# A two-layer pre-activation convolution: the order of ScalarE's work in a step, and statistics taken ahead

## The chip, the cores and the metric

The kernel runs on one core of one Trainium2 chip. The metric is the device time of one execution in microseconds. The kernel before takes 1926.62 us (median of three runs, 1925.54 to 1932.41). The profile shown here is of one execution of 1926.6 us from its first to its last instruction.

## What is computed

The input x has 8 images of 32 channels and 252 by 252 pixels, in fp32. Two layers of the same kind follow each other:

```python
def _gn(v, G=16, eps=1e-5):                  # group norm, 2 channels a group
    g = v.reshape(B_, G, C_ // G, H_, W_)
    m = jnp.mean(g, axis=(2, 3, 4), keepdims=True)
    s = jnp.var(g, axis=(2, 3, 4), keepdims=True)
    return ((g - m) / jnp.sqrt(s + eps)).reshape(v.shape)

x = x + _L0_conv_ref(_gn(x), L0_conv_weight)   # 5x5 convolution, 32 -> 32,
x = x + _L1_conv_ref(_gn(x), L1_conv_weight)   # reflected borders
```

A convolution of layer 1 on an image can start only when the mean and variance of the whole image behind layer 0 are known. The reference writes the convolution as a product of Fourier transforms; the kernel computes it directly.

## The kernel before

**Tiles.** An image is split into even and odd rows and columns, which gives four parts of 126 by 126 pixels. With 32 channels each they fill the 128 partitions. The 5x5 convolution becomes a convolution with three column taps, and along the rows a fast scheme that makes six output rows from eight transformed rows: 8 products instead of 18. One step works on a tile of 18 rows of the parts: 7 steps an image and layer, 112 steps in all.

**Phases.** `phases` (L500) lists (image, layer) pairs: layer 0 of image 0, then layer 0 of image b alternating with layer 1 of image b-1, then layer 1 of the last image: 16 phases of 7 steps. `s0` is the first step of a phase in `begin`.

**One step on each engine**, in the order of the loop at L581, for step i:

- SyncE issues all DMAs, in program order: `fetch` (L106) loads the rows of step i+4 of layer 0 into one of two halves of `xbuf`; `prepare` (L141) loads the tile `g` of step i+3 from a DRAM scratch if it is of layer 1; stores of the step before go to the scratch (L464) or to the output (L497); `input_chunk` (L267) loads parts of an image for its sums.
- GpSimd runs `differences` (L346) for step i+2: three subtractions and additions, a dependency keeps the first behind VectorE's last instruction of `transform`.
- VectorE runs `transform` (L359) for step i+1, then `finish` (L448) of step i-1, then, in `conv` (L405), s1 and d1 (L423, L424: they read m2 and a1), the pair at L431 and L432 (they read m3, m4, a3), six results y (L397), the pair at L440 and L441 (m5, m6, a5), four more y.
- TensorE runs the products m3, m4, m5, m6 of step i, then `first_products` (L401), that is m1 and m2 of step i+1, and then products 0 and 7 of step i on top of m6 and m5. Each is three matmuls of 128x378 (two instructions each in the trace, 48 a step). Products 0 and 7 write where VectorE reads m6 and m5, and so wait for the last y of L443.
- ScalarE copies a1, a3 and a5 from the PSUM (L420, L427, L437) for VectorE, and beside these it does four other kinds of work: splitting the rows of step i+3 into the tile `g` if it is of layer 0 (`prepare`, L154 to L156, through `after_1`, behind a1); the first half of the output of step i-1, or its borders and sum (`after_3`, behind a3); the second half or sum of squares (`after_5`, behind a5); sums and sums of squares of an image to come (`input_sums`, L274, also in `after_5`).

The order within an engine is the program's (`manual_schedule`, L526); every engine runs its list from top to bottom. PSUM holds seven product tiles and one small tile for statistics.

**Statistics of a phase.** `collect` (L288) adds up the partial sums, `averages` (L293) is a small matmul across partitions, `variance` (L299) ends in a square root on ScalarE, `scales` (L310) makes the factors, `scale_matrices` (L327) multiplies the phase's matrices `u` on ScalarE, `add_own` (L331) adds the residual to them on VectorE, and `find_offset` (L336) makes the offset that a1 takes as its bias. Before the change `collect` and `averages` run in step s0-2, all else in step s0-1 (`mid` and `late`, L523 and L524). The input sums of a layer-0 phase run in steps s0-7 to s0-4.

Of the kernel before, what the change touches and what calls it, by code (L numbers as in the profile page):

```python
# [46 lines left out]
F32 = mybir.dt.float32  # L47
# [5 lines left out]
P = 128  # L53
Q = 32
EPS = 1e-5
NB = 126
PB = 128
TR = 6
NT = 3
# [15 lines left out]
def tile_conv_preact_x2(ctx: ExitStack, tc: tile.TileContext, x: bass.AP, w0: bass.AP, w1: bass.AP, out: bass.AP):  # L75
# [65 lines left out]
    def prepare(b: int, l: int, T: int):  # L141

        g = gpool.tile([P, DR, NT, PB], F32, tag="g", name=f"g_{b}_{l}_{T}")
        gt[b, l, T] = g
        if l:
            nc.sync.dma_start(g[:, 0:TR], scratch[b][:, T])
            nc.sync.dma_start(g[:, TR:DR, 0 : NT - 1], scratch[b][:, T, 0:2, 1:NT])
            nc.sync.dma_start(g[:, TR:DR, NT - 1], scratch[b][:, T + 1, 0:2, 0])
            return
        t = xt.pop((b, T))  # L150
        for pc in range(2):
            cols = slice(1 - pc, W, 2)
            to = g[halves[pc], :, :, 1 - pc : 1 - pc + NB]
            nc.scalar.copy(to[:, 0:TR], t[:, 0:GR, cols].rearrange("p (t j) w -> p j t w", j=TR))  # L154
            nc.scalar.copy(to[:, TR:DR], t[:, 2:IR, cols].rearrange("p (t j) w -> p j t w", j=TR)[:, TR - 2 : TR])  # L155
        pad_columns(g.rearrange("p j t k -> p (j t k)"), 0)  # L156
# [125 lines left out]
    def output_sums(b: int, T: int, y: bass.AP, k: int):  # L282
        st = sum_slots(b, 1)
        view = y[:, 0 : GR * PB].rearrange("p (r k) -> p r k", k=PB)[:, :, 1 : 1 + NB]
        junk = spool.tile([P, GR, NB], BF16, tag="junk", name=f"junk_{b}_{T}_{k}", bufs=1)
        nc.scalar.activation(junk, view, (AF.Identity, AF.Square)[k], accum_out=st[:, k, T : T + 1])  # L286
# [44 lines left out]
    def add_own(b: int, l: int):  # L331
        u = ut[b, l]
        for pc, h in enumerate(halves):
            last["dve"] = nc.vector.tensor_add(u[h, :, 1 + pc, h], u[h, :, 1 + pc, h], own[h])

    def find_offset(b: int, l: int):  # L336
        po = pstat.tile([P, 1], F32, tag="stat", name=f"po_{b}_{l}")
        nc.tensor.matmul(po, total[l], norm.pop((b, l))[:, 1:2], start=True, stop=True)
        offset[b, l] = small.tile([P, 1], F32, tag="off", name=f"off_{b}_{l}")
        nc.scalar.copy(offset[b, l], po)  # L340


    at, vt = {}, {}
# [57 lines left out]
    def first_products(b: int, l: int, T: int):  # L401
        n = f"{b}_{l}_{T}"
        m12[b, l, T] = [product(b, l, vt[b, l, T], f, n) for f in (1, 2)]

    def conv(b: int, l: int, T: int, after_1, after_3, after_5, following):  # L405

        vs = vt[b, l, T]
        n = f"{b}_{l}_{T}"

        y = ybuf[begin[b, l] + T & 1]  # L410
        yr = y[:, 0 : GR * PB].rearrange("p (j t k) -> p j t k", j=TR, k=PB)
        yo = [yr[:, j, :, 1 : 1 + NB] for j in range(TR)]

        def temp(tag: str, bufs: int = 1):
            return mpool.tile([P, NT, NB], F32, tag=tag, name=f"{tag}_{n}", bufs=bufs)

        v = nc.vector
        m1, m2 = m12.pop((b, l, T))
        a1 = temp("a1", 2)
        nc.scalar.activation(a1, m1, AF.Identity, bias=offset[b, l])  # L420
        after_1()
        s1, d1 = temp("s1"), temp("d1")
        v.tensor_add(s1, m2, a1)  # L423
        v.tensor_sub(d1, a1, m2)  # L424
        m3 = product(b, l, vs, 3, n)
        a3 = temp("a3", 2)
        nc.scalar.copy(a3, m3)  # L427
        after_3()
        m4 = product(b, l, vs, 4, n)

        v.tensor_sub(m3, a3, m4)  # L431
        v.tensor_add(m4, m4, a3)  # L432
        for j in (1, 0, 3, 2, 5, 4):
            stt(yo[j], m3 if j % 2 else m4, 2.0**j, d1 if j % 2 else s1)
        m5 = product(b, l, vs, 5, n)
        a5 = temp("a5", 2)
        nc.scalar.copy(a5, m5)  # L437
        after_5()
        m6 = product(b, l, vs, 6, n)
        v.tensor_sub(m5, a5, m6)  # L440
        v.tensor_add(m6, m6, a5)  # L441
        for j in range(1, 5):
            stt(yo[j], m5 if j % 2 else m6, 0.5**j, yo[j])  # L443
        following()
        product(b, l, vs, 0, n, m6)
        product(b, l, vt.pop((b, l, T)), 7, n, m5)

        def finish():  # L448
            v.tensor_add(yo[0], m6, yo[0])
            stt(yo[5], m5, 0.5**5, yo[5])  # L450

        return y, finish
# [28 lines left out]
    def to_output(b: int, T: int, y: bass.AP, s: int):  # L481

        yr = y[:, 0 : GR * PB].rearrange("p (j t k) -> p j t k", j=TR, k=PB)
        if s == 0:
            ot[b, T] = opool.tile([P, half, W], F32, tag="o", name=f"o_{b}_{T}")
        o = ot[b, T] if s == 0 else ot.pop((b, T))
        o = o.rearrange("p (t j) w -> p t j w", j=TR // 2)
        js = slice(s * TR // 2, (s + 1) * TR // 2)
        dst = out[b].rearrange("ch (i r) w -> r ch i w", r=2)[:, :, GR * T : GR * (T + 1), :]
        dst = dst.rearrange("r ch (t j) w -> r ch t j w", j=TR)  # L490
        for pc in range(2):
            nc.scalar.copy(  # L492
                o[halves[s], :, :, 1 - pc : W : 2].rearrange("p t j w -> p j t w"), yr[halves[pc], js, :, 1 : 1 + NB]
            )
        for pr in range(2):
            for t in range(NT):
                nc.sync.dma_start(dst[1 - pr, :, t, js, :], o[quads[2 * s + pr], t])  # L497
# [8 lines left out]
    N = len(steps)  # L506


    chunk_load: dict = {}
    chunk_sum: dict = {}  # L510
    mid: dict = {}
    late: dict = {}
    for k, (p, s0) in enumerate(begin.items()):
        ut[p] = ubuf[(k + 1) % 2]
        if k == 0:
            continue
        b, l = p
        if l == 0:
            for c in range(NC):
                at_step = s0 - 7 + c // 2 if k > 1 else c * 5 // 8  # L520
                chunk_sum.setdefault(at_step, []).append((b, c))
                chunk_load.setdefault(at_step - 1, []).append((b, c))
        mid.setdefault(s0 - 2, []).append(p)  # L523
        late.setdefault(s0 - 1, []).append(p)  # L524

    ctx.enter_context(tc.manual_schedule())  # L526
    beside = mybir.DependencyInfo(mybir.DependencyClass.Sync, mybir.DependencyReason.DATA)
# [39 lines left out]
    add_own(0, 0)  # L567
    find_offset(0, 0)
    first_products(*steps[0])
    next(first)  # L570
    prepare(*steps[1])
    differences(nc.gpsimd, *steps[1])
# [2 lines left out]
    transform_taps(taps_at[:, 1], rows_at, rsum)  # L575
    sum_taps(1, taps_at[:, 1])

    for b, c in chunk_load.get(-1, []):
        chunks[b, c] = input_chunk(b, c)
    done = None  # L580
    for i, step in enumerate(steps):  # L581
        if i + 4 < N:
            fetch(*steps[i + 4])
        for p in mid.get(i, []):
            nc.sync.dma_start(ut[p], stored[p[1]])
            collect(*p)
        for p in late.get(i, []):
            variance(*p)
        parts = transform(*steps[i + 1]) if i + 1 < N else iter(())
        next(parts, None)  # L590
        for p in late.get(i, []):
            scales(*p)
            scale_matrices(*p)
        next(parts, None)
        for p in late.get(i, []):
            add_own(*p)
        if done:
            done[2]()
        if i + 2 < N:
            first = differences(nc.gpsimd, *steps[i + 2])  # L600
            tc.add_manual_dep(first.ins, last["dve"].ins.name, beside, reason="one reader of two operands at a time")

        def after_1():
            if i + 3 < N:
                prepare(*steps[i + 3])

        def after_3():
            if done:
                (b, l, T), y, _ = done
                if l:  # L610
                    to_output(b, T, y, 0)
                else:
                    to_scratch(b, T, y)
                    output_sums(b, T, y, 0)

        def after_5():
            if done:
                (b, l, T), y, _ = done
                if l:
                    to_output(b, T, y, 1)  # L620
                else:
                    output_sums(b, T, y, 1)
            for b, c in chunk_sum.get(i, []):
                input_sums(b, c, chunks.pop((b, c)))
            for b, c in chunk_load.get(i, []):
                chunks[b, c] = input_chunk(b, c)

        def following():
            for p in mid.get(i, []):
                averages(*p)  # L630
            for p in late.get(i, []):
                find_offset(*p)
            if i + 1 < N:
                first_products(*steps[i + 1])

        done = step, *conv(*step, after_1, after_3, after_5, following)
        if i == 1:
            make_matrices(1, rows_at, ubuf[0])
    done[2]()
# [34 lines left out]
```

## Time and profile before

| What | us |
|---|---|
| span | 1926.6 |
| TensorE busy, matmuls | 1762.5 (91%) |
| VectorE busy | 1729.5 (90%) |
| ScalarE busy | 1377.4 (71%) |
| GpSimd busy | 827.9 (43%) |
| TensorE's first product | starts at 51.9 |
| TensorE waits for VectorE's y | 88.7 in 26 waits, the longest 8.1 |
| VectorE waits at L431 for a3 | 69.9 in 15 waits, the longest 6.3 |
| ScalarE waits for m3 at L427 | 264.2 in 62 waits |
| DMA | 386.4 MB, mean 201 GB/s |

Two engines are busy nine tenths of the time and feed each other within every step, so a mean share says little here. What matters is in which steps they wait, and for whom; that is read from the timeline and from the distance of one instruction to the same instruction of the next step.

### The profile page before, as it was taken

To read this page: it belongs to the slowest core of one execution; us is meant where nothing else is said; L and a number is where in the kernel's file an instruction comes from. 1 tells how busy PE (TensorE), PEld (TensorE's weight loads), DVE (VectorE), ACT (ScalarE), POOL (GpSimd) and SP (SyncE) were. 2 spreads that over 40 slices of the span, in tenths; PEclk is the share of its full clock that TensorE was granted. 3 is DMA by queue.
4 is the path that set the end of the run, shared out by engine and by line. 5 is a ranking of instruction groups with operands and counts; after the bars stand their busy time and mean duration, and the time that the engine had idled before them with its cause. 6 is when DMAs were issued, how large, how long until landed. Compare 5 with 4: busy or idle time off the path is not lost.

```text
span 1926.6 us, 19376 instructions
## 1 busy us (share of the span) xinstructions
PE 1762.5 (91%) x5440; PEld 1041.3 (54%) x5440; DVE 1729.5 (90%) x3345; ACT 1377.4 (71%) x1649; POOL 827.9 (43%) x410
## 2 busy tenths in 40 slices
PE   0579999999999899999999999999999989999997
PEld 0345555555555455555555555555555545555554
DVE  6677899988999799988999889998899889999995
ACT  5779774988669885797847977498856988444443
POOL 5643344434444344444444434443444434444440
PEclk9789999999999999998999999999999999999999
DMA  6959768996679786797778966899767977766653
GB/s 221 237 152 223 140 142 243 285 227 139 177 232 289 171 169 196 242 262 168 147 204 302 239 147 150 245 281 226 151 180 240 278 172 156 205 173 195 180 148 87
DMA packets 225660, 386.39 MB, mean 201 GB/s; under 512 B 25488, under 2 KB 200848, under 8 KB 212624
## 3 DMA queue, kind: packets, MB, share of 16 engines
q1 hardware_dynamic: 225552, 385.16, 76.2%
q8 instruction: 42, 0.69, 0.2%
q14 instruction: 66, 0.54, 0.1%
HBM read 249.77 MB, written 135.28 MB: 200 GB/s over the span
## 4 chain that ended last, share of the span: by engine, by line
PE 55%; DVE 18%; ACT 12%; DMA 8%; issue 4%; POOL 2%; SPq 2%; ACTq 0%; DVEq 0%; POOLq 0%
PE m L387 55%; DVE y L397 8%; ACT g L154 4%; DMA x<-in_x_dram 3%; DMA out_dram<-o 1%; ACT g L155 1%; DMA g<-scratch 1%; DVE v L368 1%; ACT sx L279 1%; ACT o L492 1%; ACT sx L280 1%; DMA sx<-in_x_dram 1%; DVE m L440 1%; DVE m L432 1%; DVE m L441 1%
## 5 line engine op out<-in xcount | busy, mean ns | idle before, releaser
L387 PE MATMUL m<-v,u 128*128 128x378 f32 x5376 | 1761.3, 489 | 105.2 <-DVE y L397 88.7
L387 PEld LDWEIGHTS m<-v,u 128*128 128x128 f32 x5376 | 1031.4, 193 | 818.0 <-DVE y L397 104.7
L354 POOL TENSOR_TENSOR a<-g 128x1536 f32<-128x1536 f32 x111 | 384.4, 3463 | 1042.2 <-DVE v L368 414.7
L492 ACT COPY o<-y 64x1134 f32<-64x1134 f32 x224 | 278.3, 1242 | 12.2 <-issue 8.5
L397 DVE SCALAR_TENSOR_TENSOR y<-m,y 128x378 f32<-128x378 f32 x560 | 275.5, 542 | 2.9 <-PE m L387 2.9
L154 ACT COPY g<-x 64x2268 f32<-64x2268 f32 x112 | 256.6, 2291 | 11.9 <-DMA x<-in_x_dram 9.8
L427 ACT COPY a<-m 128x378 f32<-128x378 f32 x112 | 53.1, 474 | 266.4 <-PE m L387 264.2
L286 ACT ACTIVATE junk<-y 128x2268 bf16<-128x2268 f32 x112 | 234.7, 2096 | 1.4
L356 POOL TENSOR_TENSOR v<-g 128x768 f32<-128x768 f32 x111 | 202.6, 1825 | 0.0
L355 POOL TENSOR_TENSOR e<-g 128x768 f32<-128x768 f32 x111 | 202.6, 1825 | 0.0
L397 DVE SCALAR_TENSOR_TENSOR y<-m,d 128x378 f32<-128x378 f32 x336 | 182.1, 542 | 0.0
L397 DVE SCALAR_TENSOR_TENSOR y<-m,s 128x378 f32<-128x378 f32 x336 | 182.1, 542 | 0.0
L431 DVE TENSOR_TENSOR m<-a,m 128x378 f32<-128x378 f32 x112 | 62.2, 556 | 125.0 <-ACT a L427 69.9
L280 ACT ACTIVATE sx<-sx 128x2016 f32<-128x2016 f32 x64 | 118.9, 1857 | 19.7 <-DVE sums L277 17.4
L368 DVE SCALAR_TENSOR_TENSOR e<-g,e 128x768 f32<-128x768 f32 x112 | 108.5, 969 | 9.2 <-POOL e L355 9.2
L368 DVE SCALAR_TENSOR_TENSOR v<-p 128x384 f32<-128x384 f32 x224 | 115.2, 556 | 0.0
L368 DVE SCALAR_TENSOR_TENSOR v<-q 128x384 f32<-128x384 f32 x224 | 115.0, 555 | 0.0
L368 DVE SCALAR_TENSOR_TENSOR p<-a 128x768 f32<-128x768 f32 x112 | 107.2, 958 | 0.0
L368 DVE SCALAR_TENSOR_TENSOR q<-a 128x768 f32<-128x768 f32 x112 | 106.8, 954 | 0.0
L368 DVE SCALAR_TENSOR_TENSOR v<-a,v 128x768 f32<-128x768 f32 x112 | 106.6, 952 | 0.0
L279 ACT ACTIVATE sx<-sx 128x2016 f32<-128x2016 f32 (+1 forms) x56 | 103.5, 1848 | 0.5
L420 ACT ACTIVATE a<-m,off 128x378 f32<-128x378 f32 x112 | 63.7, 569 | 51.5 <-PE m L387 50.8
(67 smaller groups left out, 972.0 us busy)
## 6 DMA issues: line engine op xcount, KB each, us to landing
g<-scratch SPq DMA_DIRECT2D x56, 1152.0 KB, 8.9
out_dram<-o SPq DMA_DIRECT2D x672, 94.5 KB, 2.0
sx<-in_x_dram SPq DMA_DIRECT2D x56, 1008.0 KB, 5.8
x<-in_x_dram SPq DMA_DIRECT2D x88, 630.0 KB, 8.5
scratch<-y SPq DMA_DIRECT2D x112, 288.0 KB, 2.8
scratch<-y SPq DMA_DIRECT2D x112, 240.0 KB, 3.6
u<-raw SPq DMA_DIRECT2D x15, 1536.0 KB, 7.1
g<-scratch SPq DMA_DIRECT2D x56, 256.0 KB, 9.2
```

The costliest lines, as they stand in the source:

```text
L154: nc.scalar.copy(to[:, 0:TR], t[:, 0:GR, cols].rearrange("p (t j) w -> p j t w", j=TR))
L279: nc.scalar.activation(t, t, AF.Identity, accum_out=st[:, 0, c : c + 1])
L280: nc.scalar.activation(t, t, AF.Square, accum_out=st[:, 1, c : c + 1])
L286: nc.scalar.activation(junk, view, (AF.Identity, AF.Square)[k], accum_out=st[:, k, T : T + 1])
L354: first = v.tensor_sub(rows(a), rows(g[:, 3:7]), rows(g[:, 1:5]))
L355: v.tensor_add(rows(e), rows(g[:, 5:7]), rows(g[:, 1:3]))
L356: v.tensor_sub(rows(v07), rows(g[:, 6:8]), rows(g[:, 0:2]))
L368: stt = lambda o, i0, c, i1: v.scalar_tensor_tensor(o, i0, c, i1, ALU.mult, ALU.add)
L387: nc.tensor.matmul(ps, ut[b, l][:, f, b3, :], vs[f][:, :, 2 - b3 : 2 - b3 + NB], start=(b3 == 0 and onto is None), stop=(b3 == 2), skip_gr ...
L397: stt = lambda o, i0, c, i1: nc.vector.scalar_tensor_tensor(o, i0, c, i1, ALU.mult, ALU.add)
L420: nc.scalar.activation(a1, m1, AF.Identity, bias=offset[b, l])
L492: nc.scalar.copy(o[halves[s], :, :, 1 - pc : W : 2].rearrange("p t j w -> p j t w"), yr[halves[pc], js, :, 1 : 1 + NB])
```

## The change

The change reorders ScalarE's list and moves statistics. In a step, a1, a3 and a5 come as early as they can: `prepare` of step i+3 moves from behind a1 to behind a5, and a1 of the next step is issued at the end of the step (`first_copy`), behind everything else. In short, per step:

```
before:  a1, splitting, a3, output half 0, a5, output half 1, input sums
after:   a3, output half 0, a5, splitting, output half 1, input sums, a1 of the next step
```

`prepare` is also what issues the loads of a layer-1 tile; these now stand on SyncE behind the step's first stores. The input sums of an image run a step earlier (s0-8 to s0-5), `collect` and `averages` run in step s0-3 and `variance` in s0-2 (but for the second phase), `scales`, `scale_matrices`, `add_own` and `find_offset` stay in s0-1. `add_own` moves behind `finish`, and `find_offset` is split into its matmul and its copy. The aim is that VectorE does not wait for a copy that stands behind long work in ScalarE's list.

```diff
+    def first_copy(b: int, l: int, T: int):
+        m1, m2 = m12[b, l, T]
+        a1 = mpool.tile([P, NT, NB], F32, tag="a1", name=f"a1_{b}_{l}_{T}", bufs=2)
+        nc.scalar.activation(a1, m1, AF.Identity, bias=offset[b, l])
+        m12[b, l, T] = a1, m2
...
-        m1, m2 = m12.pop((b, l, T))
-        a1 = temp("a1", 2)
-        nc.scalar.activation(a1, m1, AF.Identity, bias=offset[b, l])
-        after_1()
+        a1, m2 = m12.pop((b, l, T))
...
         nc.scalar.copy(a5, m5)
-        after_5()
...
-                at_step = s0 - 7 + c // 2 if k > 1 else c * 5 // 8
-                chunk_sum.setdefault(at_step, []).append((b, c))
-                chunk_load.setdefault(at_step - 1, []).append((b, c))
-        mid.setdefault(s0 - 2, []).append(p)
-        late.setdefault(s0 - 1, []).append(p)
+                i = s0 - 8 + c // 2 if k > 1 else c * 5 // 8
+                todo(i, "sum").append((b, c))
+                todo(i - 1, "load").append((b, c))
+        early = k > 1
+        todo(s0 - 2 - early, "collect").append(p)
+        todo(s0 - 1 - early, "variance").append(p)
+        todo(s0 - 1, "scale").append(p)
...
-        for p in late.get(i, []):
-            add_own(*p)
         if done:
             done[2]()
+        for p in todo(i, "scale"):
+            add_own(*p)
...
-        done = step, *conv(*step, after_1, after_3, after_5, following)
+        finished, done = done, (step, *conv(*step, after_3, following))
+        if i + 3 < N:
+            prepare(*steps[i + 3])
+        if finished:
+            (b, l, T), y, _ = finished
+            if l:
+                to_output(b, T, y, 1)
+            else:
+                output_sums(b, T, y, 1)
+        for b, c in todo(i, "sum"):
+            input_sums(b, c, chunks.pop((b, c)))
+        for b, c in todo(i, "load"):
+            chunks[b, c] = input_chunk(b, c)
+        for p in todo(i, "scale"):
+            find_offset(*p)
+        if i + 1 < N:
+            first_copy(*steps[i + 1])
```

## The prediction

> **What bounds the kernel now.** I read the table of costliest groups first.
>
> ```profile
> L387 PE MATMUL m<-v,u 128*128 128x378 f32 x5376 | 1761.3, 489 | 105.2 <-DVE y L397 88.7
> L427 ACT COPY a<-m 128x378 f32<-128x378 f32 x112 | 53.1, 474 | 266.4 <-PE m L387 264.2
> L431 DVE TENSOR_TENSOR m<-a,m 128x378 f32<-128x378 f32 x112 | 62.2, 556 | 125.0 <-ACT a L427 69.9 <-PE m L387 54.8
> ```
>
> TensorE is busy 1761 of 1926.6 us; only its 105.2 us of idle time (plus start and end) can be won. It waits for VectorE's y (88.7), and VectorE at L431 waits 69.9 us for ScalarE's copy a3 (L427). The timeline of an undisturbed step comes next (start, length, engine, line; idle time in brackets).
>
> ```profile
> 734.65 0.56 DVE L440 TENSOR_TENSOR m<-a,m 128x378 f32<-128x378 f32 x1
> ...
> 736.49 0.58 ACT L420 ACTIVATE a<-m,off 128x378 f32<-128x378 f32 x1 [1.25 <-PE m L387]
> ...
> 744.11 0.47 ACT L427 COPY a<-m 128x378 f32<-128x378 f32 x1 [7.04 <-PE m L387]
> 744.62 0.54 DVE L423 TENSOR_TENSOR s<-m,a 128x378 f32<-128x378 f32 x1
> 746.09 0.56 DVE L431 TENSOR_TENSOR m<-a,m 128x378 f32<-128x378 f32 x1 [0.47 <-PE m L387]
> 747.92 0.47 ACT L437 COPY a<-m 128x378 f32<-128x378 f32 x1 [0.34 <-PE m L387]
> 749.89 0.56 DVE L440 TENSOR_TENSOR m<-a,m 128x378 f32<-128x378 f32 x1
> ```
>
> L440 to L440 is one step: 15.24 us. TensorE has no gap in it: 48 instructions, 0.3175 us each. I use t from L440 = 0: a1 possible from 1.84, transform from 2.76, finish from 9.05, s1 (needs a1) 9.97, a3 possible from 9.46, L431 at 11.44, a5 at 13.27 to 13.74. VectorE has 0.47 us to spare before m4 is there. TensorE's m0 may start when m2 of the next step is through, 24 instructions (7.62) after 11.44, at 19.06; it needs the last y, which ends at 18.0. So VectorE may be about 0.47 + 1.06 = **1.5 us late** before TensorE idles.
>
> Now a disturbed step.
>
> ```profile
> 612.27 0.47 ACT L437 COPY a<-m 128x378 f32<-128x378 f32 x1 [0.92 <-PE m L387]
> ...
> 615.29 1.88 ACT L279 ACTIVATE sx<-sx 128x2016 f32<-128x2016 f32 x1
> ...
> 622.64 0.56 ACT L420 ACTIVATE a<-m,off 128x378 f32<-128x378 f32 x1
> 623.22 2.31 ACT L154 COPY g<-x 64x2268 f32<-64x2268 f32 x1
> ...
> 630.17 0.47 ACT L427 COPY a<-m 128x378 f32<-128x378 f32 x1
> ...
> 630.67 0.56 DVE L431 TENSOR_TENSOR m<-a,m 128x378 f32<-128x378 f32 x1 [5.46 <-ACT a L427]
> ...
> 637.24 13.39 PE L387 MATMUL m<-v,u 128*128 128x378 f32 x36 [4.04 <-DVE y L397]
> ```
>
> Input sums (615.29 to 622.6), a1, then a tile's splitting (623.22 to 630.14, 6.92 us) stand ahead of a3: VectorE waits 5.46, TensorE 4.04. I call this A. B comes two to three steps later, where std, the scaling of u (2.86) and a splitting stand ahead of a3 (VectorE waits 3.71, TensorE 4.74). C is the start of a layer-1 phase, with no late copy, only VectorE's own extra work (TensorE waits 0.94). From the L440 times: A costs 20.10 + 16.39 - 2x15.24 = 6.0 us, B 21.23 + 16.96 - 30.48 = 7.7, C 17.44 + 14.69 - 30.48 = 1.65. The L440s from 231.70 to 1908.61 are 104 steps: 1676.9 - 104x15.24 = **92 us lost**, in six A, six B and eight C. The seven steps before (87.87 to 231.70) lose 143.8 - 106.7 = 37 more.
>
> **What the Trainium skill says.** "TensorE: Matmul & The Clock Gate", "What's actually happening": after an idle window of about 3.4 us the clock falls to half. The stretches behind the waits agree (clock is the number ahead of the DMA share): 0.67 after A, 0.50 after B, 1.00 after C's 0.94 us.
>
> ```profile
> 637.20:641.00 3.80, 3.76 (x8) 2.21 (x9) 3.80 (x7) 3.78 (x3) 0.00 (x0) 0.67 0.53 125
> 675.00:679.00 4.00, 4.00 (x7) 2.24 (x8) 4.00 (x6) 3.98 (x3) 0.00 (x0) 0.50 0.82 183
> 786.40:790.00 3.60, 3.60 (x12) 2.08 (x11) 3.60 (x6) 0.00 (x0) 0.00 (x0) 1.00 1.02 421
> ```
>
> That is why A and B cost more than their waits. "PSUM — Partial Sum Buffer", "Engine vs sequencer instructions": ScalarE's queue is strict FIFO; A agrees, a3 runs last though m3 was long done. "SBUF — State Buffer", "Who interferes with whom": a VectorE instruction with two SBUF inputs contends with a GpSimd one that reads SBUF. At 72.60 us, with GpSimd busy, L368's e took 1.63 us against 0.95.
>
> **The change part by part.** No instruction is added or removed; all is order.
>
> *Splitting moves behind a5.* ScalarE's round becomes a5, splitting 6.92, second half of output or sums (2.5 or 2.2), a1, a3, first half, a5. From a5's end at -1.5: splitting to 5.4, output half to 7.9, a1 to 8.5. Needed at 9.97: 1.4 us spare. a3 then waits for m3 (9.46), as in the quiet step. First half (2.5, or pads and sum 2.85 behind the finish at 9.96) ends by 12.85; a5 can't start before 13.27. The trace already holds a heavier case: sums of 7.76 us (600.07 to 607.83) between an output half and a1, with VectorE's s1 at 608.97 on time. Splitting's own reader is GpSimd at t 9.3, 3.9 us after its end.
>
> *Input sums one step earlier* (from s0-7..s0-4 to s0-8..s0-5, s0 the phase's first step). After the first phase no step then has both sums and splitting, and the step ahead of the first splitting has neither. The first step (s0-8) also scales u: a1 by 2.4, u when mr is there at about 6.3, to 9.2, a3 at 9.46. It fits. A goes, but for the averages' matmul.
>
> *Statistics apart.* Collect (0.17) and variance (0.51) go to earlier steps, each within 0.47 or the 1.06 behind it. Scales (0.95) and add_own (1.38) stay. The two small matmuls cost TensorE about 0.35 each as before (C: 1.65 - 0.94 = 0.7). Check on C now: 0.51 + 0.95 + 1.38 - 1.5 - 0.35 = 1.0 us of wait; measured 0.94. C after: 0.95 + 1.38 - 1.85 = 0.5, plus 0.7: **1.2**. B after: u is scaled behind a1, 8.5 to 11.4; add_own could start at 10.9, so waits 0.45; 0.45 + 2.33 - 1.85 = 0.95, plus 0.7: **1.65**. Both waits are far under 3.4 us, so no clock loss. add_own behind finish costs nothing: same VectorE sum; GpSimd starts a microsecond later, inside its 1.7 us spare (below).
>
> *Offset split.* The matmul stays, the tiny copy (0.15) moves behind splitting, just ahead of a1: within its 1.4 us.
>
> *Layer-1 tile loads.* They queue on SyncE behind the step's first stores (until t 16 to 17.5, which is 1 to 2.3 of the next step) and are wanted one step earlier: at GpSimd's t 9.3. Unmixed they land in 5.8 to 6.8 us (the 766 us group), so at 8 to 9, in time. GpSimd takes 7.05, the next transform is at 18.0, so up to 10.95 costs nothing. Taken: zero; upper end under the rivals.
>
> *First phase* (splitting and sums in the same steps whatever the order): ScalarE's sum per round is the same 21.1 us. Walking the new order, copies are about 1 us later up to the sixth step, std behind a splitting costs VectorE 3 us, and the last late a3 goes. Sum about 0, give or take 3.
>
> After: 8x1.2 + 6x1.65 = 19.5 us lost in place of 92. 1926.6 - 72.5 = **1854 us**.
>
> **The rivals.**
> 1. *Forecast*, 1854: chance 0.68. For it: sums already stand in the place where splitting goes, without a wait.
> 2. *Layer-1 loads late.* Other loads of this trace land in 9.4 to 13.7 us where sx or x loads run too. At 9.6 GpSimd overlaps the transform by 0.8 us, hidden in the 1.5; at 12.8 by 3.8, which at 1.63 for 0.95 costs 2.6, of which 1.1 shows. Take 0.5 for 56 tiles: 28 us, 1882. Against: the sx loads now stand behind the tile's in the queue. 0.14.
> 3. *B stays half*, since scaling waits behind splitting on ScalarE: with 3 us more in each of six, 1872. 0.10.
> 4. *Slower*: a1 becomes the new late copy in the 42 steps with splitting after the first phase. To cost 2.2 us each, it must be 1.4 + 1.5 + 2.2 = 5 us later than worked out: 1854 + 92 = 1946. Against: ScalarE's round is 13.9 of 15.24 us. 0.05.
> 5. *The waits only move* (two late copies per transition in other steps): about 1926. 0.03.
>
> **How the numbers follow.** Likeliest: 1854. Low 1844: all but the 14x0.7 of small matmuls goes (1926.6 - 92 + 9.8). High 1886: rival 2 with the first phase's 3. That holds cases 1 to 3 with their spread. Faster: 0.68 + 0.14 + 0.10 = 0.92; same 0.03; slower 0.05.
>
> **What would show it.** Step 1 right: no wait of L431's successor for a3 after the first phase, and 15.24 us steps through the A positions. Statistics right: TensorE waits of 0.5 and about 1 us once a phase, none over 3.4 after about 250 us, clock 1.00 in every later stretch. Loads right: GpSimd's first subtraction starts with VectorE's last transform in layer-1 steps. Wrong: VectorE waiting at s1 for a1, L368 instructions longer than 0.95 us in layer-1 phases, or GpSimd waiting for g from DMA past t 11.

## The result and the profile after

The changed kernel takes **1861.97 us** (median of four runs, 1859.93 to 1862.15), against 1929.41 for the kernel before in the same session (four runs, 1925.54 to 1932.41): a ratio of 0.965, 95% interval 0.963 to 0.967. The forecast was 1854 and the range 1844 to 1886. The direction, the mechanism and nearly the whole size were right, and 8 us of the time were not. The profiled execution spans 1860.3 us; 6.2 of the 8 us are found in it below, the rest is the distance from this span to the median (1.7 us).

The table of costliest groups after the change, for TensorE's matmuls and for VectorE's first reader of a3 (busy us, mean ns, idle us ahead of the group and what ended it):

```profile
L390 PE MATMUL m<-v,u 128*128 128x378 f32 x5376 | 1737.3, 485 | 62.6 <-DVE y L400 37.2
...
L437 DVE TENSOR_TENSOR m<-a,m 128x378 f32<-128x378 f32 x112 | 62.1, 555 | 38.9 <-PE m L390 34.3
```

VectorE's wait for the copy a3 at L437 (L431 before) fell from 69.9 us to one wait of 4.6 us, in the first phase; what ends the idle time there is now TensorE's m4. TensorE's idle time fell from 105.2 to 62.6 us. Its *busy* time fell too, from 1761.3 to 1737.3 us with the same 5376 instructions (489 to 485 ns each): there is less time at a reduced clock, 58 us in place of 113. That part of the gain is not a wait, and a count of waits alone would miss it.

The timeline of ScalarE at the splitting that stood ahead of the late a3 in A (start, length, engine, line; idle time in brackets):

```profile
619.50 0.47 ACT L443 COPY a<-m 128x378 f32<-128x378 f32 x1 [0.93 <-PE m L390]
619.87 2.30 ACT L154 COPY g<-x 64x2268 f32<-64x2268 f32 x1
...
626.79 2.50 ACT L497 COPY o<-y 64x1134 f32<-64x1134 f32 x2
629.31 0.58 ACT L411 ACTIVATE a<-m,off 128x378 f32<-128x378 f32 x1
...
631.15 0.47 ACT L433 COPY a<-m 128x378 f32<-128x378 f32 x1 [1.18 <-PE m L390]
```

Here a5 comes first, then splitting, half an output, a1, and a3 (631.15) **waits for TensorE**; VectorE and TensorE no longer wait for it. The same stretch and the transition B behind it on VectorE:

```profile
606.24 0.56 DVE L445 TENSOR_TENSOR m<-a,m 128x378 f32<-128x378 f32 x1
...
621.48 0.56 DVE L445 TENSOR_TENSOR m<-a,m 128x378 f32<-128x378 f32 x1
...
631.97 0.54 DVE L429 TENSOR_TENSOR s<-m,a 128x378 f32<-128x378 f32 x1
...
636.94 0.56 DVE L445 TENSOR_TENSOR m<-a,m 128x378 f32<-128x378 f32 x1
...
648.28 1.40 DVE L334 TENSOR_TENSOR u<-u,own 64x512 f32<-64x512 f32 x2 [0.34 <-ACT u L329]
...
654.31 0.55 DVE L445 TENSOR_TENSOR m<-a,m 128x378 f32<-128x378 f32 x1
669.00 0.56 DVE L445 TENSOR_TENSOR m<-a,m 128x378 f32<-128x378 f32 x1
```

From L445 to L445 (L440 before) is one step: 15.24 and 15.46 us where A cost 20.10 and 16.39, then 17.37 and 14.69 where B cost 21.23 and 16.96. B is now 32.06 - 30.48 = 1.6 us, or 1.8 with the 0.22 of the step ahead of it, which now has the small matmul of `averages`. TensorE's waits at B and at the next layer-1 start, C, and the clock behind the longer one (the 1.00 ahead of the DMA share):

```profile
657.19 3.12 PE L390 MATMUL m<-v,u 128*128 128x378 f32 x9 [1.09 <-DVE y L400]
...
765.24 15.19 PE L390 MATMUL m<-v,u 128*128 128x378 f32 x47 [0.66 <-DVE y L400]
```
```profile
657.20:662.00 4.80, 4.80 (x15) 2.93 (x16) 4.80 (x8) 4.17 (x8) 0.00 (x0) 1.00 0.10 24
```

For every kernel below I give two losses, both against undisturbed steps of 15.24 us and both read from the distances of L440/L445: of the **first phase** (7 steps) and of the **rest** (104 steps).

| kernel | median us | ratio to before, 95% | first phase | rest |
|---|---|---|---|---|
| before | 1929.41 | | 37.1 | 92.0 |
| after | 1861.97 | 0.965 (0.963 to 0.967) | 41.3 | 21.4 |
| order only | 1895.64 | 0.983 (0.982 to 0.985) | 42.5 | 54.1 |
| statistics and sums only | 1889.55 | 0.980 (0.979 to 0.982) | 36.9 | 53.4 |
| sums only | 1891.55 | 0.981 (0.980 to 0.982) | 37.6 | 55.1 |
| collect late | 1854.78 | 0.962 (0.961 to 0.964) | 34.5 | 21.4 |
| loads early | 1861.93 | 0.966 (0.964 to 0.967) | 41.4 | 21.4 |
| slack 1 | 1874.72 | 0.973 (0.971 to 0.974) | 41.2 | 33.8 |
| slack 2 | 1957.16 | 1.015 (1.013 to 1.017) | 41.4 | 116.5 |
| spread | 1848.42 | 0.958 (0.957 to 0.960) | 36.1 | 13.6 |
| order with loads | 1888.87 | 0.980 (0.978 to 0.981) | 42.2 | 44.3 |
| spread with loads | 1843.09 | 0.956 (0.955 to 0.957) | 34.7 | 9.4 |
| fill | 1835.23 | 0.952 (0.951 to 0.953) | 27.1 | 9.4 |

The runs of before beside the experiments had medians of 1927.55 to 1927.98; the ratios are to the runs of the same session. The change moves the two losses by +4.2 and -70.6, that is -66.4 us; the two spans (1926.6 and 1860.3) differ by 66.3. The first-phase losses of kernels with the same first phase lie up to 1.6 us apart.

### The profile page after: what moved, and what is told of

The parts are those of the page before. It is cut to its first block, busy times and chain, and to the rows that moved or that the text cites. A ratio compares the mean times of both kernels' runs of the same rounds, so it can differ in the third digit from the quotient of the medians.

```text
span 1860.3 us, 19459 instructions
## 1 busy us (share of the span) xinstructions
PE 1738.6 (93%) x5440; PEld 1030.4 (55%) x5440; DVE 1729.0 (93%) x3345; ACT 1379.1 (74%) x1649; POOL 829.0 (45%) x410
## 4 chain that ended last, share of the span: by engine, by line
PE 66%; DVE 12%; ACT 8%; DMA 6%; POOL 3%; issue 3%; SPq 1%; DVEq 0%; ACTq 0%; POOLq 0%
PE m L390 66%; DVE y L400 5%; DMA sx<-in_x_dram 4%; ACT g L154 2%; DVE v L371 1%; DMA x<-in_x_dram 1%; ACT o L497 1%; POOL a L357 1%; DMA scratch<-y 1%; ACT u L329 1%; ACT g L155 1%; ACT junk L286 1%; POOL rows L185 1%; DVE m L438 1%; DVE m L445 1%
## 5 line engine op out<-in xcount | busy, mean ns | idle before, releaser
L390 PE MATMUL m<-v,u 128*128 128x378 f32 x5376 | 1737.3, 485 | 62.6 <-DVE y L400 37.2
L390 PEld LDWEIGHTS m<-v,u 128*128 128x128 f32 x5376 | 1020.3, 191 | 762.5 <-DVE y L400 49.7
L155 ACT COPY g<-x 64x756 f32<-64x756 f32 x112 | 100.0, 893 | 0.0
L437 DVE TENSOR_TENSOR m<-a,m 128x378 f32<-128x378 f32 x112 | 62.1, 555 | 38.9 <-PE m L390 34.3
```

The costliest lines, as they stand in the source:

```text
L390: nc.tensor.matmul(ps, ut[b, l][:, f, b3, :], vs[f][:, :, 2 - b3 : 2 - b3 + NB], start=(b3 == 0 and onto is None), stop=(b3 == 2), skip_gr ...
```

## The experiments

The theory: the gain comes from short copies that no longer stand behind long work (A), and from statistics that no longer meet the late copy (B) or are spread over more steps (C). The rivals were late loads of layer-1 tiles, the late a1, and B staying half. A further question was where the 6 us of the miss sit.

### The three parts alone

*Order only* is the changed kernel with sums and statistics at their old steps:

```diff
-                i = s0 - 8 + c // 2 if k > 1 else c * 5 // 8
+                i = s0 - 7 + c // 2 if k > 1 else c * 5 // 8
...
-        early = k > 1
+        early = False
```

> The changed kernel with ScalarE's new order alone: input sums again in s0-7 to s0-4, collect in s0-2 and variance in s0-1 for every phase. My theory: transition A is gone all the same, because sums and splitting now stand in different rounds of ScalarE. In B std stands behind a splitting in the step that needs it, so VectorE waits about 2.7 us for it at the reciprocal and is about 5.5 us late with the rest, which leaves TensorE some 3.7 us of wait and a clock drop; about 5.7 us a B in place of 1.7, and C back at 1.65. In sum 47 us lost after the first phase in place of 21: about 1886 us against 1862. Rival (the statistics carry the gain): over 1905.

*Sums only* is the kernel before with the input sums one step earlier:

```diff
-                at_step = s0 - 7 + c // 2 if k > 1 else c * 5 // 8
+                at_step = s0 - 8 + c // 2 if k > 1 else c * 5 // 8
```

> The kernel before with one thing changed: the input sums run in s0-8 to s0-5. My theory: this alone removes A, six times 6.0 us: about 1893 us against 1929, with VectorE's longest wait at L431 after the first phase falling from 5.5 to 3.7 us (B). Rival (A is due to the order alone): no change, since a splitting still stands ahead of a3.

*Statistics and sums only* has that edit, and takes `collect`, `averages` and `variance` a step ahead, on the order of before:

```diff
-        mid.setdefault(s0 - 2, []).append(p)
+        early = k > 1
+        mid.setdefault(s0 - 2 - early, []).append(p)
+        var_at.setdefault(s0 - 1 - early, []).append(p)
         late.setdefault(s0 - 1, []).append(p)
...
-        for p in late.get(i, []):
+        for p in var_at.get(i, []):
             variance(*p)
```

> The kernel before with the statistics moved alone: input sums in s0-8 to s0-5, collect in s0-3, variance in s0-2; ScalarE's order in a step as before. My theory: A is gone too, since the step ahead of the first splitting has no sums, so a3 behind a1 and a splitting comes at about t 9.4; B stays at about 7 us (scaling, a1, splitting, a3), C falls to 1.2. In sum 52 us lost in place of 92: about 1888 us against 1929, and a first phase as in the kernel before. So each half alone wins about 40 of the 67 us, as A is counted in both. Rival (the order carries the gain): over 1915. Rival (the parts add): the savings of this and of the order alone sum to 67 and not to 80.

Measured: 1895.64, 1891.55 and 1889.55 us; the last two are within 2 us of what was expected. *A* goes by moving the sums alone: the rest's loss falls from 92.0 to 55.1, which is 36.8 us. The six A had lost 33.9 of it (five of 5.9 to 6.0, and one of 4.1, behind which the clock did not fall); the other 2.9 come out of B. The new order alone removes A too, so the two gains do not add up. *B* needs both. With the statistics ahead but the old order, B's two steps are 20.74 and 16.78 us, 7.0 lost of 7.7, because scaling and splitting still stand ahead of a3 and TensorE's wait (4.3 to 4.7) still costs clock. What that kernel gains over sums only is small: C's wait is 0.64 in place of 0.93. The pieces of the new order (splitting, a1, `add_own`, the split offset) were not tried apart.

Order only came out 9.6 us above what I expected. Most of that is rival 2, where it was not looked for. The timeline of GpSimd and, below it, that of VectorE in that kernel:

```profile
404.35 3.48 POOL L357 TENSOR_TENSOR a<-g 128x1536 f32<-128x1536 f32 x1 [12.37 <-DMA g<-scratch]
```
```profile
409.64 2.57 DVE L371 SCALAR_TENSOR_TENSOR e<-g,e 128x768 f32<-128x768 f32 x1 [0.58 <-POOL e L358]
```

The last layer-1 tile of a phase arrives late, GpSimd runs beside VectorE's transform, and its e takes 2.57 us where it takes 0.95. The waits of GpSimd for g total 99.0 us in that kernel, against 43.9 in the changed one. SyncE's own waits show a part of it: the second load of this tile is issued 2.5 us late, when a load of x has landed. Why the same queue order hurts here and not there was not isolated.

### Loads early

The changed kernel with the loads of a layer-1 tile issued at their old place, ahead of the convolution:

```diff
+        if i + 3 < N and steps[i + 3][1]:
+            prepare(*steps[i + 3])
         finished, done = done, (step, *conv(*step, after_3, following))
-        if i + 3 < N:
+        if i + 3 < N and not steps[i + 3][1]:
             prepare(*steps[i + 3])
```

> The changed kernel with the loads of a layer-1 tile issued ahead of the step's first stores again; ScalarE's order is the same. My theory: GpSimd's waits for g from DMA (43.9 us in five waits, first subtraction up to 2 us late) go away, and the time stays within 2 us of 1862, because a delay of GpSimd of less than 1.7 us reaches no one. Rival (late loads cost time): 5 to 10 us less.

Measured: 1861.93 us, the same. This line of the waits of the changed kernel (us in total, times, longest) is gone with the edit, and no time goes with it:

```profile
POOL a L357 <- DMA g<-scratch: 43.9, 5, 9.2
```

So those waits are hidden, and rival 2 falls for the changed kernel. (The tile takes a median of 8.8 us from issue to landing at the old place, 5.8 at the new one.)

### Order with loads early

Order only with the same edit, which removes the late tile from it:

> The kernel with ScalarE's new order alone, and in addition the loads of a layer-1 tile issued ahead of the step's first stores. My theory of what its B cost beyond the worked 5.7 us: the last layer-1 tile of a phase landed late behind loads of x and of an image's parts, GpSimd started 2 to 4 us late and ran beside transform, whose first instruction took 2.6 us in place of 0.95. With the loads early the step ahead of B goes back to 15.24 to 15.5 us and the time falls by 6 x 1.0 to 1.5, about 8 us, to 1887 (the 1886 that I had worked out). Rival (the rest is the clock behind the 3.7 us waits): within 2 us of 1895.

Measured: 1888.87 us, 6.8 less than order only, where about 8 were expected. The rest's loss is 44.3 in place of 54.1, but 3.4 of these 9.8 us are two falls of the clock behind B that this execution was spared. The late tile had cost order only some 6 to 7 us. Order alone then brings 47.7 us in the rest, statistics and sums 38.5, both 70.6. The parts sum to 86.2. They don't add up for two opposite reasons: A (33.9) is counted in both, and some 18 us (70.6 - 86.2 + 33.9), nearly all of B, come only with both. These are sums over single executions, and the four runs of this kernel lie 7.7 us apart (the profiled one is the fastest), so 18 can be up to 5 too low.

This kernel also shows what an idle TensorE costs by its clock. In B it waits 3.48 us ahead of 443.89 and 3.62 us ahead of 663.25. The step behind is 14.69 us in the first case and 16.39 in the second: what looks like 0.14 us more of wait cost 1.7 us. The Trainium skill ("TensorE: Matmul & The Clock Gate", "What's actually happening") gives about 3.4 us for an idle window that is *free-running*, so it need not start with the wait. The traces bear this out. In all thirteen of them each stretch at half clock begins on a fixed grid of 3.41 us. Here are the two waits on this grid (busy time of TensorE, and behind it the clock, 1.00 or 0.50):

```profile
438.78:442.19 3.41, 1.63 (x6) 1.00 1.11 244
442.19:445.61 3.42, 1.72 (x6) 1.00 0.08 23
445.61:449.02 3.41, 3.41 (x12) 1.00 0.31 72
...
660.65:664.06 3.41, 0.81 (x3) 1.00 0.01 3
664.06:667.47 3.41, 3.41 (x7) 0.50 0.14 31
```

The first wait lies half in one window and half in the next, and the clock stays. Of the second 2.60 us fall into one window, and the next window runs at half clock. That section speaks of an idle window; a window wholly without work is not needed here. After the first 250 us of the thirteen traces, no window at full clock that was idle for less than 0.54 of its length was followed by half clock, and every one that was idle for more than 0.59 was. So some 2 us of idle time in one window are enough. A wait of 3.00 us shows it in the changed kernel, at its very end, where TensorE waits for the last y:

```profile
1841.90:1845.32 3.42, 0.43 (x2) 1.00 0.63 146
1845.32:1848.73 3.41, 3.40 (x6) 0.50 0.46 110
```

In the kernel before a wait of 3.86 us (ahead of 1323.12), split 0.56 and 0.57 over two windows, left the clock at 1.00. Since an execution's waits fall on the grid as they happen to, the same kernel may lose more or less clock each time; that this makes the 7.7 us between the four runs is likely, but only one of them was profiled.

### Collect late

The first phase: `collect` behind `finish` and `add_own` in VectorE's list, where it had stood ahead of the transform.

```diff
-            collect(*p)
...
             add_own(*p)
+        for p in todo(i, "collect"):
+            collect(*p)
```

> The changed kernel with collect issued behind finish on VectorE instead of ahead of transform. My theory of what I missed in the first phase: in step 5 VectorE stands 8.5 us at collect for the last input sums, which ScalarE now does behind a splitting, and the whole transform waits behind it. With collect behind finish s1 of that step is at about 188.6 (when a1 is there) in place of 195.4: 5 to 7 us less, about 1856 us. Nothing changes after the first phase. Rival (ScalarE alone bounds the first phase, and the wait only moves to s1 or to std): 1862 as it is.

Measured: 1854.78 us, as expected. Here is the reason, on VectorE in the changed kernel, around the fifth step:

```profile
188.14 0.17 DVE L290 TENSOR_REDUCE tot<-sums 128x2 f32<-128x16 f32 x1 [8.47 <-ACT sx L280]
188.23 0.95 DVE L371 SCALAR_TENSOR_TENSOR e<-g,e 128x768 f32<-128x768 f32 x1
```

An instruction of 0.17 us waits 8.47 us for the last input sum, and the whole transform waits behind it. The kernel before had this wait as well:

```profile
181.41 0.17 DVE L290 TENSOR_REDUCE tot<-sums 128x2 f32<-128x16 f32 x1 [2.25 <-ACT sx L280]
```

There the sums stood ahead of the splitting of the next step; now they stand behind the one of this step. With `collect` moved, that step takes 16.4 us in place of 23.2, and the first phase loses 34.5 us in place of 41.3. The rest does not change.

### Slack 1 and slack 2

Behind each splitting after the first phase, three or seven copies of a 128x320 tile onto itself are added on ScalarE, to measure how late a1 may come:

```diff
             prepare(*steps[i + 3])
+            if i >= 14 and steps[i + 3][1] == 0:
+                spare = rsum.rearrange("p r k c -> p (r k c)")
+                for _ in range(3):
+                    nc.scalar.copy(spare, spare)
```

> The changed kernel with three extra copies on ScalarE (an unused 128x320 tile onto itself, about 1.1 to 1.3 us together) between the splitting and the second half of the output, in the 42 steps with a splitting behind the first phase. My theory: a1 has 1.4 us and ScalarE's round 1.3 us to spare, so the time stays within 2 us of 1862. Rival (a1 is already at its limit): each added microsecond is paid, about 1862 + 42x1.2 = 1912.

> As before with seven copies, about 2.5 to 3.0 us. My theory: ScalarE's round becomes 16.4 to 16.9 us in the steps with output sums and 15.9 to 16.4 in the others, over 15.24, so a group of seven such steps falls behind by 7 to 10 us, of which 1.4 us of a1's spare and 1.5 us of VectorE's are free: TensorE waits 4 to 7 us a group, 24 to 42 us in six groups: 1886 to 1904, with VectorE waiting at s1 for a1. Rival (ScalarE is off the path): 1862.

Both were missed. With three copies (1.44 us) two steps of each group of seven are still 15.24 us, so the spare of 1.4 us that the prediction gave a1 is there, about as worked out. But the time rose by 12.8 us. Scaling u stands behind a1, and `add_own` waits for u, in the steps that had no spare. Before B, in slack 1, on ScalarE and on VectorE:

```profile
644.09 1.44 ACT L635 COPY rsum<-rsum 128x320 f32<-128x320 f32 x3
...
648.55 2.85 ACT L329 ACTIVATE u<-u,mr 128x3072 f32<-128x3072 f32 x1
```
```profile
651.43 1.41 DVE L334 TENSOR_TENSOR u<-u,own 64x512 f32<-64x512 f32 x2 [1.82 <-ACT u L329]
```

The wait of 0.34 has become 1.82, the step 18.85 us in place of 17.37: 1.5 for 1.44 added, six times, 9.0 us. The rest is 3.4 us in steps with output sums, two in each group, which are 0.2 to 0.36 us longer. ScalarE has 0.35 to 0.7 us of idle time left in them, ahead of a5; what makes them longer was not isolated.

Seven copies took 3.40 us (I had allowed 2.5 to 3.0), and the kernel is 1.5% slower than before. One line of its waits (us in total, times, longest):

```profile
DVE s L429 <- ACT a L411: 62.3, 38, 5.9
```

Rival 4, then, is a real mechanism: a1 becomes the late copy. In the changed kernel it is 1.4 us away from it. In this run TensorE also waited for a1 itself, 31.1 us in 13 waits of up to 2.9. B's waits went to 4.65 us, and the clock fell behind each.

### Spread, spread with loads, fill

*Spread* is collect late with collect and variance another step earlier and `scales` and `scale_matrices` a step ahead of `add_own`:

```diff
-        todo(s0 - 2 - early, "collect").append(p)
-        todo(s0 - 1 - early, "variance").append(p)
-        todo(s0 - 1, "scale").append(p)
+        todo(s0 - 2 - 2 * early, "collect").append(p)
+        todo(s0 - 1 - 2 * early, "variance").append(p)
+        todo(s0 - 1 - early, "scale").append(p)
+        todo(s0 - 1, "own").append(p)
...
```

> A version meant to beat both: the changed kernel with collect behind finish, and for every phase but the second collect in s0-4, variance in s0-3, scales and the scaling of u in s0-2, add_own and the offset in s0-1. My theory: VectorE's extras are then 0.95 in one step and 1.38 in the next, both inside its 1.5 us with 0.54 us won back each step, so TensorE's waits of 0.66 and 0.9 to 1.1 us at the 14 transitions after the first phase go: 11 us less than with collect behind finish alone, about 1845 us; what stays is 0.7 us of small matmuls a transition. Rival (scaling u behind a splitting makes a3 late in s0-2 and moves the wait there): as with collect behind finish alone, about 1856.

Measured: 1848.42. The extra work of VectorE in a B now fits in two steps' spare, and the rest loses 13.6 us. What stays above the floor (the small matmuls, 9.4 us) is mostly a late tile again, now behind the load of u (e takes 1.5 to 2.2 us in five steps; in one of them u landed at 603.90 and the tile at 609.42). *Spread with loads* adds the edit of loads early:

> Collect behind finish, the statistics spread over four steps, and the loads of a layer-1 tile issued ahead of the step's first stores. My theory: the one step a phase that took 16.1 to 16.8 us with the statistics spread, where the last layer-1 tile landed late behind the load of u, goes back to 15.5: 6 x 0.6 to 1.3 us, about 1843 us in place of 1848. Rival (that step is long because of the variance on VectorE): no change.

Measured: 1843.09, the rest's loss 9.4 us. That is 14 x 0.67, the small matmuls of the statistics alone, which I had taken as the low end of the range. *Fill* adds one thing for the first phase: in step 1 the input sums are issued at the head of what follows a3, where they had stood at the end of the step.

```diff
         def after_3():
+            if i == 1:
+                add_sums()
...
```

> The last one, and in step 1 alone the input sums placed ahead of the borders of step 0's result, where ScalarE otherwise stands some 10 us waiting for VectorE's y. My theory: the first phase is bound by ScalarE's total from step 1 on, so 7.8 us of sums in a hole of 10 bring a1 of step 2 forward by about 7.8 us, and VectorE's waits there (5.9 at s1, then 4.6 at a3) shrink: 5 to 8 us less, about 1837 us. Rival (TensorE's slow clock or GpSimd sets the first phase): within 2 us of 1843.

Measured: **1835.23 us**, the fastest, 0.952 (0.951 to 0.953) of the time before. In the changed kernel ScalarE idles in step 1, waiting for a result y whose borders it has to fill:

```profile
109.04 0.25 ACT L137 COPY y<-y 64x36 f32<-64x36 f32 x1 [9.95 <-DVE y L400]
...
121.13 1.87 ACT L279 ACTIVATE sx<-sx 128x2016 f32<-128x2016 f32 x1
```

The sums that run from 121.13 on, ahead of the next a1, fit into those 9.95 us. In fill they do, and the borders wait 1.29 in place of 9.95:

```profile
99.38 1.89 ACT L279 ACTIVATE sx<-sx 128x2016 f32<-128x2016 f32 x1
...
108.53 0.26 ACT L137 COPY y<-y 64x36 f32<-64x36 f32 x1 [1.29 <-DVE y L400]
```

On VectorE the changed kernel has two waits in the step that follows,

```profile
129.47 0.55 DVE L429 TENSOR_TENSOR s<-m,a 128x378 f32<-128x378 f32 x1 [5.92 <-ACT a L411]
...
135.06 0.56 DVE L437 TENSOR_TENSOR m<-a,m 128x378 f32<-128x378 f32 x1 [4.59 <-ACT a L433]
```

and fill has one, of 2.87 us at a3. That step falls from 25.2 to 17.5 us.

## Why the prediction was right, and where it was not

- **A goes**: right. 15.24 us for the step that had 20.10, no wait for a3 after the first phase. The reason is there twice over: the earlier sums alone do it (sums only), and the order alone does it too.
- **B**: 1.65 predicted, 1.7 measured as the mean of six (with the 0.22 of the step ahead of each). TensorE waits 0.91 to 1.09 us (0.95 predicted), and `add_own` waits 0.16 to 0.34 for u (0.45 predicted). Rival 3, with 3 us more in each B, falls.
- **C**: 1.2 predicted, 1.4 measured (+0.22 and +1.69 in two steps, -0.54 in the third). The wait is 0.66 and not 0.5. Eight times 0.17 (1.37 for 1.2) is 1.4 of the 1.9 us by which the rest (21.4 for 19.5) was short; B makes the other 0.5.
- **Clock**: right for the waits of about 1 us that were forecast. After about 250 us the clock is 1.00 up to 1845 us, and the matmuls' busy time fell by 24.0 us. The bound of 3.4 us for a wait was too high: at the end the clock falls behind one of 3.00 us, as in the kernel before. And the opening sentence, that only TensorE's 105.2 us of idle time (plus start and end) can be won, does not hold: 24.0 of the 66.3 us came out of its busy time. The sum was not harmed by it, as it was made from lengths of steps.
- **a1's spare of 1.4 us**: right in the quiet steps (slack 1). What I had not seen is that in B the same queue has none: the 1.44 us added there landed on `add_own`.
- **Layer-1 loads at no cost**: right (loads early, no difference): GpSimd waited for g in five steps, and nothing waited for GpSimd there. It does not hold for every plan (order only, spread).
- **First phase, "Sum about 0, give or take 3"**: wrong, and this is the failed term. It is +4.2 us. I walked the copies and priced std behind a splitting at 3 us; the wait at the reciprocal behind it measures 2.18. What the walk left out are `collect` and the transform behind it, a wait of 8.47 us in place of 2.25. The first four steps together changed by 0.3 us; the fifth to seventh went from 55.4 to 59.3. I had asked what is queued behind a waiting instruction for ScalarE's copies and not for VectorE's instruction of 0.17 us, too short to stand among the costliest groups. With it moved (collect late) the first phase is 2.6 us *better* than before. Whether the reordering itself is a gain there isn't shown, since this also takes away the wait of 2.25 that the kernel before had.

Of the 6.2 us in the span, 4.2 are this term and 1.9 the slightly larger C and B.

## What to carry to other kernels

On an in-order engine that does short copies for others and long side work, put each copy first when its input arrives and the side work behind the last of them; then ask of *every* instruction that waits for that side work, however short, what stands behind it on its own engine. Two remedies for one wait do not add up (A), and another wait may need both (B): try each alone before both are credited. A measured spare holds for the steps in which it was measured; the few steps with extra work in the same queue have their own.

## What was not expected of the hardware

- TensorE's clock fell after waits of 3.00, 3.56, 3.62 and 3.65 us and not after 3.48, 3.51, 3.67 and 3.86. The length of the wait alone doesn't decide; what does is whether some 0.6 of one window of the 3.41 us grid is idle. Where it fell behind B in order with loads, it cost 1.7 us over the next step.
- ScalarE's added copies of 128x320 took 0.486 us each in a row (3.40 us for seven), each reading what the one ahead wrote. I had counted 0.36 to 0.43.
- A tile that comes late costs VectorE and not GpSimd: e, with two operands in SBUF, took 2.57 us beside GpSimd's work in place of 0.95 (1.63 in the prediction's instance), while GpSimd's own instructions kept their length (3.48 and 1.82 us). The Trainium skill ("SBUF — State Buffer", "Who interferes with whom") names the contention; its size here is up to 1.6 us a tile.
- Where a1 was very late, TensorE itself waited for ScalarE (31.1 us in slack 2). It is presumably the PSUM tile of m1 that only a1 frees; this was not tested apart.
